# A selective scan whose chunk groups, prefetch distance and state copies are rearranged

## The chip, the core and the metric

The kernel runs on one core of a Trainium2 chip. The metric is the device time of one execution in microseconds (us), lower is better. The median of three runs of the kernel before is 34833.05 us (34830.49 to 34833.85). Four engines compute: TensorE (PE in the profile, its weight loads PEld), VectorE (DVE), ScalarE (ACT) and GpSimd (POOL). SyncE (SP) issues the DMA transfers. Each engine runs its own list of instructions strictly in order; between engines, an instruction waits on semaphores until what it needs is done.

## The reference

Two layers work on an image batch of 8 x 56 x 56 x 192 in float32. The first (a gated Toeplitz convolution) is not touched. The second is a vision state-space block: a projection to 384 channels, a 3x3 depthwise convolution, and then a selective scan along eight directions over the 3136 pixels, with N = 16 states per channel:

```python
dA = jnp.exp(dl[..., None] * A)
h = dA * h + (dl * ul)[..., None] * bl[:, :, None, :]
y = jnp.einsum('bkdn,bkn->bkd', h, cl)
```

Here `dl` is delta (a softplus of a projection of the pixel), `ul` the pixel, `bl` and `cl` the projected B and C, k the direction. Afterwards the eight directions are added, normalised, gated with silu and projected. The scan is the bulk of the work: 8 images x 8 directions x 3136 steps x 384 channels x 16 states.

## The kernel before

**Units.** For each image the scan stage cuts a direction into 50 chunks of 63 pixels and the 384 channels into three blocks of 128. One chunk of one channel block is a *unit*: 8 x 150 = 1200 units per image, 9600 in all. Units of the three channel blocks are dealt out in turn (block d lags d chunks behind), so the unit before in the same chain, whose last state is needed, is three units back.

**What one unit costs each engine.** PE makes delta*u*B for all states as a product of the turned delta*u with a diagonal image of B (`products`, L723, into one of three PSUM buffers `bx`). ACT makes exp(delta*A) ahead of time (`exps`, L702, 16 instructions per *block*, one for each state, over all the block's chunks at once, into one of four buffers `da`), and copies the chain's last state into the first column of `bx` (`before`, L734, the "state copy"). DVE runs the recurrence (`scan`, L738). POOL multiplies by C (`times_c`, L749, into `hc`). PE adds the 16 states by transposing them onto one another (`sums`, L835, eight instructions per unit, into `yps`); every fourth unit ACT copies `yps` out (L869, tile `yt`, the "output copy"), and SP stores it.

**Groups and blocks.** The chunks of a direction form groups of 8, and a last group of 2 (50 = 6 x 8 + 2). A group's front work is shared: load (`load`), projection on PE and ACT (`project`, `projected`), delta (`steps`, `stepped`, one `softplus` on ACT, L591, which brings another activation table in and the exponential's back, L702 ACT_TABLE_LOAD), and per pair of chunks delta*u on POOL (`product`, L614), its transpose (`turn` on PE, `turned` on ACT: tile `dut`), a copy with halves exchanged (`swapped`: `dus`), the diagonal of B back from DRAM (`diagonal_in`: `bd`) and C broadcast to all partitions (`broadcast`: `cbt`). The 2-chunk group has special functions (`all_steps`, `all_stepped`). A block is the four (in the last group two) chunks of one channel block that share 16 exponentials.

**The order is written out by hand.** A loop runs over steps t, one unit each; at step t the lists of all engines get, in this order: products of unit t+2; the store of earlier outputs; state copies of units t to t+2, as far as not done; sums of unit t-4; the output copy where t is a multiple of 4; planned ACT work; exponentials; the scan of unit t; planned PE work; times C of unit t-1; planned POOL and SP work; more exponentials; at last planned "late" work (the softplus). `plan` sets the steps of the front work relative to the group's first unit f. Exponentials are dealt out by a budget: each step adds 2.4 to `credit` (a debt stays, a surplus lapses), an exponential costs 0.4, a state copy 0.2, an output copy 0.35, planned ACT work 0.5, a softplus 3.0. While credit is left, exponentials are issued as far as their `da` buffer is free by the order of units (`may_exp`). Without regard to credit, all that remain of a block are issued at the step before its first unit (`must_exp`):

```python
            def may_exp(t):
                if not exps:
                    return False
                P = exps[0][0]
                return P.i < 4 or t > blocks[P.i - 4].end

            def must_exp(t):
                return bool(exps) and t >= exps[0][0].first - 1
```

## Time and profile before

| | us |
|---|---|
| median of three runs | 34833.05 |
| profiled execution | 34832.71 |
| its span | 34830.9 |
| PE busy | 30277.1 (87%) |
| DVE busy | 23676.0 (68%) |
| ACT busy | 22543.9 (65%) |
| POOL busy | 22154.0 (64%) |

The span divides into a first layer (up to about 3650 us) and eight rounds, one per image, of a scan stage and a shorter stage around it. In the trace the scans of the third image run from 11519 to 14950 us, 3431 us for 1200 units; the eight images are alike. PE's busy time counts pipelined matrix products by modelled ends, so its 87% says less than it seems to. The page's line of granted clocks (PEclk) is the share of full speed at which TensorE was allowed to run; in this kernel it moves between half and full in stretches of some microseconds.

### The profile page before, as it was taken

The numbers are of one execution on the slowest core, as the hardware profiler recorded it, in microseconds if no ns is written. First come the engines' busy times: TensorE is split into PE (matmuls) and PEld (weight loads), VectorE is DVE, ScalarE is ACT, GpSimd is POOL, SyncE is SP. The second block draws the span as 40 slices with busy tenths as digits, with TensorE's granted clock in tenths as the row PEclk, the third lists the DMA queues.
The fourth block names the chain that finished last, engine by engine and source line by source line (L and its number), as shares of the span: only waits on it lengthen the run. The fifth ranks groups of instructions, "written<-read, shape, count | busy, mean of one in ns | idle before, by whom it ended". The sixth has DMA issues, their size and how long they took to land. (4 is left out here: it accounts for less than half of the span.)

```text
span 34830.9 us, 473357 instructions
## 1 busy us (share of the span) xinstructions
PE 30277.1 (87%) x156976; PEld 16476.7 (47%) x156976; DVE 23676.0 (68%) x13460; ACT 22543.9 (65%) x58955; POOL 22154.0 (64%) x11592
## 2 busy tenths in 40 slices
PE   8999888888888888888888888888888888888888
PEld 5555444444444444444444444444444444444444
DVE  3443577747776677747776677747776677747776
ACT  2332577737775677737775577747775577737775
POOL 0000687838875588738885588838885588837885
PEclk9999999989999899989999899989999899989999
DMA  3222444444444444444444444444444444444445
GB/s 76 58 65 54 115 126 129 127 129 127 127 129 135 121 127 127 128 129 127 127 127 137 122 127 126 129 129 127 127 126 136 122 128 127 127 129 128 127 127 145
DMA packets 5635667, 4228.55 MB, mean 121 GB/s; under 512 B 3712080, under 2 KB 5007888, under 8 KB 5625680
## 3 DMA queue, kind: packets, MB, share of 16 engines
q1 hardware_dynamic: 5600080, 4191.04, 45.6%
q8 instruction: 1262, 20.68, 0.2%
q10 hardware_dynamic: 33152, 7.23, 0.2%
q14 instruction: 1173, 9.61, 0.1%
HBM read 3389.38 MB, written 507.38 MB: 112 GB/s over the span
## 5 line engine op out<-in xcount | busy, mean ns | idle before, releaser
L738 DVE TENSOR_TENSOR_SCAN h<-da,bx 128x1024 f32<-128x1024 f32 x9600 | 21246.8, 2270 | 6552.5 <-ACT bx L734 4705.1
L749 POOL TENSOR_TENSOR hc<-h,cbt 128x1008 f32<-128x1008 f32 x9600 | 20512.7, 2169 | 4271.5 <-DVE h L738 3956.8
L702 ACT ACTIVATE da<-delta,A_logs 128x252 f32<-128x252 f32 (+1 forms) x39936 | 16435.2, 489 | 5.6
L723 PE MATMUL bx<-bd,dus 63*128 63x504 f32 x19200 | 11288.7, 670 | 2682.7 <-DVE h L738 2679.7
L835 PEld LDWEIGHTS yps<-ident,hc 128*126 128x126 f32 x76800 | 8599.6, 145 | 7854.7 <-issue 4818.3
L723 PE MATMUL bx<-bd,dut 63*128 63x504 f32 x19200 | 11296.7, 670 | 81.6 <-DVE h L738 66.7
L835 PE MATMUL yps<-ident,hc 128*126 128x128 f32 x76800 | 10942.6, 288 | 266.2 <-ACT yt L869 235.7
L723 PEld LDWEIGHTS bx<-bd,dus 63*128 63x128 f32 x19200 | 2995.8, 195 | 4689.6 <-DVE h L738 3606.0
L734 ACT COPY bx<-h 128x16 f32<-128x16 f32 x9408 | 1695.0, 181 | 4555.2 <-PE bx L723 3257.6
L723 PEld LDWEIGHTS bx<-bd,dut 63*128 63x128 f32 x19200 | 2995.9, 195 | 1271.5 <-issue 920.5
L614 POOL TENSOR_TENSOR du<-delta,xs 128x378 f32<-128x378 f32 x1600 | 1587.1, 992 | 1550.1 <-ACT bx L734 1377.5
L425 POOL MEMSET xp<- 128x58 f32 x12 | 1.3, 188 | 3409.8 <-DMA bd<-none 3409.7
L869 ACT COPY yt<-yps 126x256 f32<-126x256 f32 x2400 | 891.0, 371 | 1917.0 <-PE yps L835 1794.0
L989 POOL COPY xo<-xp 128x672 f32<-128x672 f32 x98 | 70.5, 749 | 2849.7 <-ACT xp L972 2849.7
L547 PE MATMUL px<-xs,xpw 128*64 128x504 f32 (+1 forms) x2688 | 1367.9, 593 | 195.2 <-DMA xs<-xo 195.2
L578 PE MATMUL pd<-pxs,dtw 13*128 13x504 f32 x2304 | 1294.4, 641 | 17.8 <-ACT delta L587 10.7
L623 PE MATMUL pt<-ident,du 128*128 128x128 f32 x4800 | 816.5, 279 | 411.1 <-POOL du L614 405.5
L965 PE MATMUL pc<-xp,dg 128*128 128x448 f32 x2646 | 1019.6, 538 | 0.0
L972 ACT ACTIVATE xp<-pc,conv_b 128x448 f32<-128x448 f32 x147 | 93.5, 636 | 1345.8 <-PE pc L965 1345.6
L1109 DVE SCALAR_TENSOR_TENSOR y<-xc,dsum,ysum 128x224 f32<-128x224 f32 x336 | 125.4, 443 | 1128.6 <-PE ysum L1090 1128.6
L623 PEld LDWEIGHTS pt<-ident,du 128*128 128x128 f32 x4800 | 559.5, 142 | 529.0 <-POOL du L614 517.2
L631 ACT COPY dut<-pt 128x384 f32<-128x384 f32 x1600 | 766.2, 479 | 25.3 <-PE pt L623 24.9
(137 smaller groups left out, 16295.3 us busy)
## 6 DMA issues: line engine op xcount, KB each, us to landing
cbt<-cd SPq DMA_DIRECT2D x1600, 1008.0 KB
bd<-bd SPq DMA_DIRECT2D x3200, 256.0 KB
dus<-dut SPq DMA_DIRECT2D x3200, 96.0 KB
yk<-yt SPq DMA_DIRECT2D x3584, 84.0 KB
yt<-yt SPq DMA_DIRECT2D x9408, 31.5 KB
xs<-xo SPq DMA_DIRECT2D x384, 756.0 KB
xo<-xo SPq DMA_DIRECT2D x168, 672.0 KB
bd<-pxs SPq DMA_DIRECT2D x3200, 3.9 KB
```

The source lines that it names most:

```text
L547: nc.tensor.matmul(self.px[:, : self.n], weights[self.k][0][:, d], self.xs[:, d], start=(d == 0), stop=(d == NB - 1),)
L578: nc.tensor.matmul(self.pd[:, : self.n], weights[self.k][1][:, d * 128 : (d + 1) * 128], self.pxs[0 : R + 1], start=True, stop=True,)
L614: nc.gpsimd.tensor_mul(self.du[:, :, :, :W], self.delta[:, :, part].rearrange("p d (c t) -> p d c t", t=W), xs[:, :, part].rearrange("p d ...
L623: nc.tensor.transpose(self.pt[:, d * 128 : (d + 1) * 128], self.du[:, d].rearrange("p c t -> p (c t)"), ident,)
L702: yield nc.scalar.activation(da[:, : self.nc, n, 1:], src.rearrange("p (c t) -> p c t", t=W), AF.Exp, scale=an[:, G.k, self.d, n : n + 1],)
L723: nc.tensor.matmul(self.bx[:, r, :, 1:], G.dut[p][q ^ r][rows, self.d * 128 : (self.d + 1) * 128], G.bd[p][rows, q, :, :W], start=True, st ...
L734: nc.scalar.copy(self.bx.rearrange("p r n t -> p (r n) t")[:, :, 0], src)
L738: nc.vector.tensor_tensor_scan(self.h.rearrange("p n t -> p (n t)"), das[self.P.i % 4][:, self.slot].rearrange("p n t -> p (n t)"), self.b ...
L749: nc.gpsimd.tensor_tensor(hc, self.h[:, :, 1:], self.G.cb[self.c // 2][:, :, q * W : (q + 1) * W], ALU.mult)
L835: nc.tensor.matmul(yps[:, t // 4 % 2, t // 2 % 2], lhsT=hcs[t // 2][:, n].rearrange("p c t -> p (c t)"), rhs=ident, start=(n == 0), stop=( ...
L869: nc.scalar.copy(y, yps[:, s // 4 % 2])
L965: nc.tensor.matmul(pc, dg[:, d, j, :], xp[:, d, t * RT + dy : t * RT + dy + RT, dx : dx + HW], start=(j == 0), stop=(j == 8),)
```

## The change

- The groups become 8, 6, 8, 6, 8, 6, 8 chunks (SIZES) instead of six of 8 and one of 2; a block is half a group, four or three chunks. The special functions of the 2-chunk group go. The exponentials of a direction become 42 blocks of 16 instead of 39, in all 43,008 instructions instead of 39,936, over 252 or 189 elements a partition instead of 252 or 126.
- delta*u, its transpose, exchanged copy and diagonals are planned three steps earlier (s = f - 11 + 6p instead of f - 8 + 6p); the pool `blk` that holds them gets four buffers instead of three. The exchanged copy is issued one step after the diagonals instead of before them. The softplus is at f - 14 instead of f - 10; the projection at f - 27 instead of f - 24 (f - 30 for the 2-chunk group).
- The state copy is issued one unit ahead instead of two: at step t for units t and t+1, after the sums, and after up to two exponentials that are issued whatever the credit. Ahead of a softplus, the copies of the next two units are issued.

```diff
-NG = -(-NC // GC)
+SIZES = (8, 6, 8, 6, 8, 6, 8)
-            blk = st.enter_context(tc.tile_pool(name="blk", bufs=3))
+            blk = st.enter_context(tc.tile_pool(name="blk", bufs=4))
...
                 def softplus(self):
-                    v = self.delta.rearrange("p d l -> p (d l)")
-                    nc.scalar.activation(v, v, AF.Softplus)
+                    nc.scalar.activation(self.delta, self.delta, AF.Softplus)
...
                 def plan(self, at):
                     f = self.first
-                    if self.last:
-                        x = f - 30
-                        at("PE", f - 24, self.all_steps)
-                        at("late", f - 23, self.all_stepped)
-                    else:
-                        x = f - 24
-                        for d, s in enumerate((f - 18, f - 16, f - 12)):
-                            at("PE", s, self.steps, d)
-                            at("ACT", s + 1, self.stepped, d)
-                        at("late", f - 10, self.softplus)
-                    at("SP", x - 12, self.load)
+                    x = f - 27
+                    at("SP", f - 35, self.load)
...
-                    at("SP", x + 3, self.to_dram)
+                    at("SP", x + 4, self.to_dram)
+                    for d, s in enumerate((f - 21, f - 19, f - 15)):
+                        at("PE", s, self.steps, d)
+                        at("ACT", s + 1, self.stepped, d)
+                    at("late", f - 14, self.softplus)
                     for p in range(self.npr):
-                        at("SP", x + 3 + p, self.diagonal_out, p)
-                        s = f - 8 + 6 * p
+                        at("SP", x + 4 + p, self.diagonal_out, p)
+                        s = f - 11 + 6 * p
                         at("POOL", s - 1, self.product, p)
                         at("PE", s, self.turn, p)
                         at("ACT", s + 1, self.turned, p)
-                        at("SP", s + 1, self.swapped, p)
                         at("SP", s + 1, self.diagonal_in, p)
+                        at("SP", s + 2, self.swapped, p)
...
                 def __init__(self, G, s, d):
-                    self.nc = min(SC, G.nch - s * SC)
+                    self.nc = G.sc
...
+            def befores(t, n):
+                nonlocal credit
+                for U in units[max(t, 0) : max(t + n, 0)]:
+                    if not U.ready and (U.prev is None or U.prev.h is not None):
+                        U.before(U.prev)
+                        credit -= 0.2
+
...
-                for i in range(t, t + 3):
-                    U = unit(i)
-                    if U is not None and not U.ready and (U.prev is None or U.prev.h is not None):
-                        U.before(U.prev)
-                        credit -= 0.2
                 s = t - 4
                 if unit(s) is not None:
                     if s % 2 == 0:
...
                         sums(s - 1, 1)
                         hcs.pop(s // 2)
+                for i in range(2):
+                    if may_exp(t):
+                        one_exp()
+                befores(t, 2)
...
                 while credit > 0.2 and may_exp(t):
                     one_exp()
+                if ("late", t) in plan:
+                    befores(t + 1, 2)
                 credit -= 3.0 * do("late", t)
```

## The prediction

> **What bounds the kernel now.** I read the costliest groups first, then busy time by windows inside one scan stage, then the timeline at its worst and at a quiet place.

> ```profile
> L738 DVE TENSOR_TENSOR_SCAN h<-da,bx 128x1024 f32<-128x1024 f32 x9600 | 21246.8, 2270 | 6552.5 <-ACT bx L734 4705.1
> L734 ACT COPY bx<-h 128x16 f32<-128x16 f32 x9408 | 1695.0, 181 | 4555.2 <-PE bx L723 3257.6
> L869 ACT COPY yt<-yps 126x256 f32<-126x256 f32 x2400 | 891.0, 371 | 1917.0 <-PE yps L835 1794.0
> ```

> DVE's scan is the spine of a stage; of its 6552 us of idle time 4705 end with ScalarE's state copy, so the copy arrives late.

> ```profile
> 11948.00:12062.00 114.00, 83.64 (x374) 43.29 (x373) 64.51 (x30) 65.10 (x178) 69.45 (x36) 0.84 0.34 94
> 12130.00:12376.00 246.00, 238.97 (x1306) 127.89 (x1306) 222.39 (x101) 214.09 (x579) 226.21 (x117) 1.00 0.56 149
> ```

> Columns: PE, PEld, DVE, ACT, POOL busy (count), granted clock, DMA share, GB/s. Around a change of direction 30 scans take 114 us (3.8 us a unit, clock 0.84); in the middle 101 take 246 us (2.44, clock 1.00) with PE busy 97%. A direction takes 3431/8 = 428.9 us; at 2.44 throughout it would be 366. So 63 us per direction, 4.0 ms in 64, are lost around the 2-chunk group. There the timeline reads:

> ```profile
> 11982.66 0.19 ACT L734 COPY bx<-h 128x16 f32<-128x16 f32 x1 [2.06 <-PE bx L723]
> 11982.79 0.57 ACT L587 COPY delta<-pd 128x504 f32<-128x504 f32 x1
> 11983.26 5.64 ACT L702 ACTIVATE da<-delta,A_logs 128x252 f32<-128x252 f32 x14
> 11988.81 0.17 ACT L734 COPY bx<-h 128x16 f32<-128x16 f32 x1
> 11988.99 8.82 DVE L738 TENSOR_TENSOR_SCAN h<-da,bx 128x1024 f32<-128x1024 f32 x4 [7.77 <-ACT bx L734]
> 11991.33 1.20 PE L723 MATMUL bx<-bd,dus 63*128 63x504 f32 x1 [4.58 <-DVE h L738]
> 11993.31 1.97 PE L835 MATMUL yps<-ident,hc 128*126 128x128 f32 x8
> 11996.44 1.10 PE L835 MATMUL yps<-ident,hc 128*126 128x128 f32 x8
> ```

> Fourteen exponentials that were overdue go out in one run (5.64 us; (5.64 - 0.50)/13 = 0.395 us each), DVE waits 7.77 us, PE in turn 4.58 us, and then works at half speed (sums 1.97 instead of 1.10 us). So the disease is a *run of exponentials ahead of a scan*; the idle PE and its lower clock make it worse. Last, the quiet stretch:

> ```profile
> 4521.20 1.09 PE L835 MATMUL yps<-ident,hc 128*126 128x128 f32 x8
> 4522.33 0.37 ACT L869 COPY yt<-yps 126x256 f32<-126x256 f32 x1 [0.82 <-PE yps L835]
> 4511.48 1.28 ACT L591 ACT_TABLE_LOAD   x1
> 4512.77 1.46 ACT L591 ACTIVATE delta<-delta 128x1512 f32<-128x1512 f32 x1
> 4514.41 15.54 DVE L738 TENSOR_TENSOR_SCAN h<-da,bx 128x1024 f32<-128x1024 f32 x7 [1.95 <-ACT bx L734]
> ```

> The output copy starts 0.04 us after the sums *of its own step* end (4521.20 + 1.09), although they write the other half of `yps`: it stands behind them. A softplus costs DVE 1.95 us.

> **The change, part by part.** Times below are per direction unless said otherwise; E is the end of a scan.

> *Front work three steps earlier, four buffers, order of its DMAs.* Nothing is added: 25 pairs a direction as before, two transfers each for diagonals and exchanged copy. They have little to give: idle time on all engines that a diagonals' transfer ended around `bx` is 64 us in the whole run. On SP the diagonals pass the exchanged copy, which stands one step longer; both have seven steps (over 15 us) before use. On POOL delta*u goes two steps behind the softplus instead of one, so its 2.8 to 3.9 us wait there goes; POOL's demand (2.14 + 0.99/6 = 2.30 us a unit) is under PE's. I take 0, bounds -1 us a direction (64/64) to +1 (one late transfer, 0.56 us issue).

> *Exponentials.* 252 elements cost 0.395; 126 elements 0.295 (five in 1.57); so 189 about 0.345 (estimate between the rows). 384 x 0.395 + 288 x 0.345 = 251 us against 576 x 0.395 + 48 x 0.295 = 242: 9 us more ACT work, beside a PE that needs 2.07 + 0.31 = 2.38 us a unit (products 1.05, sums 1.02; projections, delta and transposes 7.4 us in 24 units). Cost 0 as work. Their *place* is what counts.

> *The budget.* In 18 units of a 6-group: 96 exponentials x 0.4 + 18 x 0.2 + 4.5 x 0.35 + 7 x 0.5 + 3 = 50.1 against 18 x 2.4 = 43.2. An 8-group: 52.3 against 57.6. A pair loses 1.6, and a debt stays. So the budget never allows anything; all that runs ahead is the forced two a step, and the rest falls due at once. The program of the changed kernel shows this all the way (copies C with unit number, then what ACT does up to the next; S softplus, Y output copy):

> ```
> C192 dut 2exp | C193 Y 8exp 2exp | C194 delta 2exp | C195 2exp | C196 delta 2exp | C197 Y 8exp 2exp
> C200 delta | C201 S 2exp Y 8exp 2exp | C202 2exp ...   (8-group)
> C218 delta | C219 S 4exp | C220 2exp | C221 Y 8exp 2exp | C222 dut 14exp 2exp   (6-group)
> ```

> Runs of six and more stood before about nine times a direction; now each of 42 blocks begins with 8 or 14 overdue ones (10 or fewer behind a softplus). For half of the 8-groups (the alignment shifts by two with each 6-group) they stand behind the output copy.

> *State copy one unit ahead.* Before, a run of exponentials stood behind the copy of unit t+2, which waits for the scan t-1; now behind that of t+1, which waits for t-2. So a run has one scan more of cover, 2.2 us. That is all that the move gives; with 42 runs a direction instead of nine it is used up, and behind an output copy, which waits for products of t+2 as before, it does not exist.

> *Eight behind the output copy* (unit t+1, step t). From E(t-1): 0.1 to PE, product 1.05, sums 1.09, 0.04, copy 0.27 to the next instruction, eight exponentials 3.27, 0.09 to the scan: 5.9. Then the scans t+1 to t+3, 2.26 + 2 x 2.2 = 6.7 (2.2: eleven scans in 24.30 us), until the next such E: 12.6 us per four units, where 2.44 gives 9.8.

> *Eight without it.* The copy, one ahead, waits for E of three units back: 0.1 + 1.16 + 0.13 + 3.27 + 0.09 = 4.75, then two scans 4.5: 9.2; PE's 9.5 is longer. With the projections' steps in a row, 10.0.

> *Softplus in an 8-group.* Two copies stand ahead of it now, the second waits for its products and holds the softplus behind it by 1.4; and the next scan needs it *and* ten exponentials: 1.4 + 4.0 (two loads and the softplus) + 3.95 + 0.3 = 9.6, then 4.5: 14.1 per four units.

> *6-group.* Softplus, 30 exponentials x 0.345 and small copies fall in one chain of five units: 1.4 + 4.1 + 10.3 + 0.9 = 16.7 against 11.0. A second chain: 1.4 + 2.8 + 0.8 + 0.4 + 5.5 + 0.2 = 11.1 against 6.6. 18 x 2.2 + 5.7 + 4.5 = 49.8, with output copies 50.5.

> *Half clock.* Without it: 2 x (5 x 12.6 + 14.1) + 2 x (5 x 9.5 + 14.1) + 3 x 50.5 = 428.9, by chance what a direction takes now. But PE idles: after the product and sums of t+1 up to 3.9 us behind the output copy, 5 us at a softplus, 3.9 and 4.5 in a 6-group; before, 4.58 was enough. Its price from the run of 14: 0.1 + 1.16 + 0.13 + 0.47 + 5.6 + 0.1 = 7.6 after the E at 11979.0 (four scans from 11972.40 on, of which the third ended there) would be 11986.6; the scan came 2.4 later. Bounds 0 and 2.4 for each; I take 1.2 per output-copy four (work of PE next to it often fills the gap), 1.5 per softplus, 2 per chain of a 6-group: 2 x (5 x 13.8 + 15.6) + 2 x (5 x 10 + 15.6) + 3 x 54.5 = 464. That is +35 us, x 64 = 2240 us on the profiled 34832.7 (the median is 0.3 more): **37,070 us**.

> [...]

> **Rivals.**
> - *No throttling* (clock 1.00 as in the middle): 428.9 a direction, about 34,830. For it: waits at PE of 1 to 2 us in the middle left the clock at 1.00. Against it: 4.58. With errors of +-9 us a direction, 34,250 to 35,400.
> - *Faster: the output copy does not hold the eight.* If it found its sums long done, eight would cost 10.0 everywhere: 464 - 2 x 19 = 426; without the clock's loss then (-25) 401, so 33,050. It decides from 2.8 us less per such four. Against it: 1794 of the copy's 1917 us idle end with the sums.
> - *Faster: the middle's pace everywhere*, 366 + 3 a direction: 31,000. Speaks for it that the 2-chunk group is gone; against it the runs of eight and fourteen.
> - *Worse throttling*: every event pays 2.4, output-copy groups at 15 per four units: 490, so 38,750.

> **How the numbers follow.** Main case 0.70 (35,400 to 38,600); no throttling 0.11 (faster 0.04, same 0.02, slower 0.05); output copy free 0.08; middle's pace 0.04; worse throttling 0.07. Faster by over 0.2% (about what a measurement of this kernel can tell from no change) 0.16, same 0.02, slower 0.82. The range 34,600 to 38,600 leaves out the two faster cases and most of the worst.

> **What would show it.** Right: DVE's idle time spread over whole stages instead of around direction changes; most of it ended by exponentials (`da`) rather than by the state copy; runs of eight at once after an output copy; PEclk below 9 tenths throughout; four units at 12.5 to 15 us in every second 8-group. Wrong: clock 1.00 and 2.4 us a unit in 8-groups; or the output copy starting right after its state copy.

## The result, and the profile after

The changed kernel takes 39,644.4 us (median of four runs, 39,637.2 to 39,664.8) against 34,832.3 for the kernel before (34,830.5 to 34,833.9). The ratio is 1.138, with a 95% interval of 1.136 to 1.140. Slower was predicted (chance 0.82), but the size was not: 37,070 us was forecast and the range ended at 38,600. A scan stage of one image takes 4030 us instead of 3430, or 504 us a direction instead of 429; the prediction had 464.

The page of the kernel after, its costliest groups (busy time and mean ns of one, then the idle time of the engine just before them and what ended most of it), with the line of granted clocks:

```profile
span 39636.9 us, 475157 instructions
PE 32472.0 (82%) x156976; PEld 17579.7 (44%) x156976; DVE 23680.0 (60%) x13460; ACT 22984.7 (58%) x62219; POOL 22269.5 (56%) x11592
PEclk9998888888888888888888888888888888888888
...
L714 DVE TENSOR_TENSOR_SCAN h<-da,bx 128x1024 f32<-128x1024 f32 x9600 | 21257.8, 2269 | 11361.9 <-ACT da L678 9433.6
L853 ACT COPY yt<-yps 126x256 f32<-126x256 f32 x2400 | 888.2, 370 | 6335.9 <-PE yps L813 6329.9
L710 ACT COPY bx<-h 128x16 f32<-128x16 f32 x9408 | 1653.7, 176 | 2550.0 <-PE bx L699 2376.6
```

The busy time of DVE is what it was (23,680 us); ACT has 441 us more work. What grew is DVE's idle time ahead of the scans: 11,362 us instead of 6552, 4810 more, which is the whole difference of the two times. Before, most of it ended with the state copy; now 9434 of it ends with an exponential (`da`). The output copy, which sits on ACT ahead of such exponentials, waited 1794 us for its sums before; now it waits 6330.

Two groups of 8 chunks of the third image by windows (PE, PEld, DVE, ACT, POOL busy with counts, granted clock, DMA share, GB/s), the first with its blocks' starts behind output copies, the second without, and then the whole scan stage:

```profile
13334.00:13431.00 97.00, 77.22 (x315) 40.27 (x316) 52.92 (x24) 51.16 (x140) 54.86 (x28) 0.76 0.34 80
13493.00:13563.00 70.00, 60.97 (x300) 32.31 (x301) 52.85 (x24) 49.24 (x137) 52.31 (x28) 0.90 0.49 119
12718.00:16750.00 4032.00, 3284.33 (x15614) 1737.25 (x15615) 2657.49 (x1202) 2666.26 (x7440) 2755.41 (x1405) 0.87 0.41 107
```

Twenty-four scans take 97 us in the one group and 70 in the other. In the first the clock is at 0.76. Over the run (from the start of the scan three units ahead of a group to the same place of the next group, means):

| us per group | predicted, full clock | predicted in all | measured |
|---|---|---|---|
| 8 chunks, output copy ahead of the block starts | 77.1 | 84.6 | 93.7 |
| 8 chunks, without | 61.6 | 65.6 | 70.4 |
| 6 chunks | 50.5 | 54.5 | 59.0 |

A direction has two, two and three of them. (In the prediction's sum without the half clock four units of the second kind stand at 9.5 us, in its whole sum at 10.0; it gave the 0.5 to the projections' steps, so 2.5 of the 4.0 us between 61.6 and 65.6 are no clock.) The shortfall of 41 us is 2 x 9.1 + 2 x 4.8 + 3 x 4.5: it lies in all three kinds, and most in the first. The timeline shows the kind that lost most: four units, from one output copy to the next (called a *four* below), of the first group (start, duration, engine, in brackets the idle time before it and what ended it):

```profile
13345.09 0.37 ACT L853 COPY yt<-yps 126x256 f32<-126x256 f32 x1 [2.78 <-PE yps L813]
13345.36 4.06 ACT L678 ACTIVATE da<-delta,A_logs 128x252 f32<-128x252 f32 x10
13348.72 8.82 DVE L714 TENSOR_TENSOR_SCAN h<-da,bx 128x1024 f32<-128x1024 f32 x4 [5.49 <-ACT da L678]
13351.06 1.21 PE L699 MATMUL bx<-bd,dus 63*128 63x504 f32 x1 [3.11 <-DVE h L714]
...
13353.05 1.97 PE L813 MATMUL yps<-ident,hc 128*126 128x128 f32 x8
13354.94 1.62 PE L577 MATMUL pd<-pxs,dtw 13*128 13x378 f32 x2
13356.50 1.21 PE L699 MATMUL bx<-bd,dut 63*128 63x504 f32 x1
...
13358.48 1.97 PE L813 MATMUL yps<-ident,hc 128*126 128x128 f32 x8
...
13361.62 1.10 PE L813 MATMUL yps<-ident,hc 128*126 128x128 f32 x8
...
13362.76 0.37 ACT L853 COPY yt<-yps 126x256 f32<-126x256 f32 x1 [3.97 <-PE yps L813]
13363.02 4.06 ACT L678 ACTIVATE da<-delta,A_logs 128x252 f32<-128x252 f32 x10
```

The output copy, ten exponentials of which the scan needs the first eight, the scan 3.63 us after the copy: that is the predicted chain. PE restarts after 3.1 us of idleness and 2.34 us after the scan's start. Its three products, three sums and a delta projection then stand between it and the next output copy, all up to the last product and sums at half speed (sums 1.97 instead of 1.09). That copy comes 11.70 us after the restart, and the next such scan (13366.38) 17.66 us after the first, where the prediction had 13.8.

### The profile page after: what moved, and what is told of

It is laid out like the page before. It is cut to its first block, busy times and chain, and to the rows that moved or that the text cites. A ratio compares the mean times of both kernels' runs of the same rounds, so it can differ in the third digit from the quotient of the medians.

```text
span 39636.9 us, 475157 instructions
## 1 busy us (share of the span) xinstructions
PE 32472.0 (82%) x156976; PEld 17579.7 (44%) x156976; DVE 23680.0 (60%) x13460; ACT 22984.7 (58%) x62219; POOL 22269.5 (56%) x11592
## 5 line engine op out<-in xcount | busy, mean ns | idle before, releaser
L678 ACT ACTIVATE da<-delta,A_logs 128x252 f32<-128x252 f32 x43008 | 17071.6, 474 | 5.4
L699 PE MATMUL bx<-bd,dus 63*128 63x504 f32 x19200 | 12353.3, 728 | 4953.1 <-DVE h L714 4945.7
L813 PEld LDWEIGHTS yps<-ident,hc 128*126 128x126 f32 x76800 | 9318.2, 153 | 8623.7 <-issue 6599.5
L699 PE MATMUL bx<-bd,dut 63*128 63x504 f32 x19200 | 12361.1, 728 | 859.9 <-DVE h L714 845.5
L813 PE MATMUL yps<-ident,hc 128*126 128x128 f32 x76800 | 11784.0, 302 | 176.5 <-ACT yt L853 163.1
L699 PEld LDWEIGHTS bx<-bd,dus 63*128 63x128 f32 x19200 | 3210.9, 209 | 6203.1 <-DVE h L714 5560.1
L699 PEld LDWEIGHTS bx<-bd,dut 63*128 63x128 f32 x19200 | 3211.2, 209 | 3077.5 <-issue 1769.7
L577 PE MATMUL pd<-pxs,dtw 13*128 13x504 f32 (+1 forms) x2688 | 1597.9, 678 | 36.0 <-ACT dut L612 18.2
L586 ACT COPY delta<-pd 128x504 f32<-128x504 f32 (+1 forms) x1344 | 713.4, 531 | 1116.9 <-PE pd L577 1116.8
```

The lines of the kernel that those rows point to most:

```text
L577: nc.tensor.matmul(self.pd[:, : self.n], weights[self.k][1][:, d * 128 : (d + 1) * 128], self.pxs[0 : R + 1], start=True, stop=True,)
L678: yield nc.scalar.activation(da[:, : self.nc, n, 1:], src.rearrange("p (c t) -> p c t", t=W), AF.Exp, scale=an[:, G.k, self.d, n : n + 1],)
L699: nc.tensor.matmul(self.bx[:, r, :, 1:], G.dut[p][q ^ r][rows, self.d * 128 : (self.d + 1) * 128], G.bd[p][rows, q, :, :W], start=True, st ...
L813: nc.tensor.matmul(yps[:, t // 4 % 2, t // 2 % 2], lhsT=hcs[t // 2][:, n].rearrange("p c t -> p (c t)"), rhs=ident, start=(n == 0), stop=( ...
```

## The experiments

The prediction's own theory (the letter A in the quoted expectations, each of which says what it stands for) is: a budget that stays in debt lets exponentials fall due eight and fourteen at a time, these runs hold the scan up, most of all behind an output copy, and TensorE, idle meanwhile (3.1 us in the four above), loses half its clock (0.50 granted for 10.24 us there, 0.76 in the mean of the group). Its rivals are the parts of the change themselves (earlier front work, new place of the state copy, size of groups). Times of 34,814 to 34,881 us were measured for the kernel before beside these runs; each ratio is to those.

### The budget's debt taken away

An exponential is charged by its size (0.3 for three chunks, 0.4 for four), so that an 18-unit group sums to 50.1 - 96 x 0.1 = 40.5 against its 43.2, and the debt of the run-in (the steps ahead of the first unit) is dropped. The two edits were not timed apart, but the program's own loop tells how many of an image's 5376 exponentials fall due without credit: 2938 in the changed kernel, 2875 with the debt dropped alone (it comes back), 322 with the charge by size alone, 301 with both. So nearly all of it is the charge.

```diff
-                credit -= 0.4
+                credit -= 0.1 * exps[0][0].nc
...
-                credit = min(credit, 0.0) + 2.4
+                credit = min(credit, 0.0) * (t > 0) + 2.4
```

> The changed kernel, with one thing else: an exponential instruction is charged by its size (0.4 for four chunks, 0.3 for three) and the debt is cleared at step 0, so that the budget holds and exponentials are issued ahead (4 to 7 a step) instead of falling due eight and fourteen at a time. Theory A (overdue runs of exponentials, sharpened by PE's lower clock): the stalls of 3.5 to 9.5 us before block starts vanish, the clock is back near 1.00 in the stage, a direction takes 366 to 390 us instead of 504: 30,800 to 32,300 us. Rival B (the grouping itself, or the front work three steps earlier, costs the time through more blocks, 3072 more exponentials and crowded PE steps): it stays over 37,000. Rival C (the state copy issued late is the cost, since it leaves one scan of cover): over 36,000.

Measured: 32,218.8 us, 0.925 of before (0.924 to 0.926), clock 0.965 over the run. With all the rest of the change in place, two numbers in the budget are worth 7426 us. The groups take 61.3, 60.3 and 47.5 us. The line of its scan, from its page:

```profile
L714 DVE TENSOR_TENSOR_SCAN h<-da,bx 128x1024 f32<-128x1024 f32 x9600 | 21278.6, 2270 | 3913.1 <-ACT bx L710 1445.9
```

Of the 11,362 us of DVE's idle time 3913 are left, and exponentials no longer end most of it. The budget is the cause of the loss, not the new groups as such.

### The parts of the change alone

The front work three steps earlier, with four buffers and the new order of its DMAs, on the kernel before; the 2-chunk group's projection moves with it.

```diff
-            blk = st.enter_context(tc.tile_pool(name="blk", bufs=3))
+            blk = st.enter_context(tc.tile_pool(name="blk", bufs=4))
...
-                        x = f - 24
-                        for d, s in enumerate((f - 18, f - 16, f - 12)):
+                        x = f - 27
+                        for d, s in enumerate((f - 21, f - 19, f - 15)):
...
-                        at("late", f - 10, self.softplus)
+                        at("late", f - 14, self.softplus)
...
-                        s = f - 8 + 6 * p
+                        s = f - 11 + 6 * p
...
-                        at("SP", s + 1, self.swapped, p)
                         at("SP", s + 1, self.diagonal_in, p)
+                        at("SP", s + 2, self.swapped, p)
```

> The kernel before with the front work alone moved: delta*u, transpose, exchanged copy and diagonals three steps earlier in four buffers, exchanged copy behind the diagonals, projection and delta three and softplus four steps earlier (the 2-chunk group's projection and delta three earlier too); groups, state copies and budget as before. Theory A: the waits lie with runs of exponentials, which stay; 34,830 within 300 us. Rival B (the crowded or shifted front work costs, or its earlier transfers gain): more than 500 us off.

Measured: 34,920.9 us, 1.0023 (1.0013 to 1.0033). That is 1.2 us a direction (0.7 to 1.8 by the interval), about the bound of 1 that the prediction gave, and nothing beside the 75 in question.

The new place of the state copy alone, on the kernel before:

```diff
-                for i in range(t, t + 3):
-                    U = unit(i)
-                    if U is not None and not U.ready and (U.prev is None or U.prev.h is not None):
-                        U.before(U.prev)
-                        credit -= 0.2
...
+                for i in range(2):
+                    if may_exp(t):
+                        one_exp()
+                befores(t, 2)
...
+                if ("late", t) in plan:
+                    befores(t + 1, 2)
```

> The kernel before with the new order of state copies alone (one unit ahead, behind the sums and two forced exponentials, two copies ahead of a softplus); groups of 8 and 2 and front work as before. Theory A: the nine long runs of a direction remain but have one scan more of cover (2.2 us each and part of the clock's loss), the softplus stall of 2 us goes: 25 to 45 us a direction less, 32,000 to 33,300 us. Rival C (the later copy costs): slower than 34,830.

Measured: 33,612.6 us, 0.9649 (0.9633 to 0.9665). The gain is 19 us a direction. The prediction said one scan of cover, 2.2 us, for each long run of exponentials, of which the kernel before has about nine: 20 us. The range on record had been set deeper, and the time missed it by 300 us. That 19 and 20 agree does not show the price per run, since the edit also brings the two forced exponentials and the copies ahead of a softplus, and the trace has fewer long runs: 464 of six and more instead of 544.

The opposite: the changed kernel with the old order of copies, with neither the forced exponentials ahead of the copies nor the early copies at a softplus.

```diff
+                befores(t, 3)
                 s = t - 4
...
-                for i in range(2):
-                    if may_exp(t):
-                        one_exp()
-                befores(t, 2)
...
-                if ("late", t) in plan:
-                    befores(t + 1, 2)
```

> The changed kernel with the state copies issued as before (units t to t+2 ahead of the sums, no two forced exponentials, no copies ahead of the softplus); groups, front work and buffers as changed. The program then issues nearly all blocks as runs of sixteen. Theory A: a run of sixteen costs 1.4 + 6.3 + 0.2 - 2.2 = 5.7 us and 2.5 for the clock, 42 times a direction: 330 + 42 x 8.2 = 675 us, so 50,000 us (45,000 to 54,000). Rival C (the later state copy is what costs): at or under 39,640, towards 35,000.

Measured: 50,393.1 us, 1.447 (1.444 to 1.450). Without the two forced ones a step, all sixteen exponentials of a block fall due at once, 2328 times, behind a copy that waits for a scan. From its page:

```profile
PEclk9997777877777777877778777777778777787777
...
L714 DVE TENSOR_TENSOR_SCAN h<-da,bx 128x1024 f32<-128x1024 f32 x9600 | 21201.3, 2268 | 22172.6 <-ACT bx L710 21999.2
```

DVE waits longer than it works. So the new order of copies with its two forced exponentials, which the prediction credited with 2.2 us a run, is worth 10,700 us in the changed kernel; the harm comes from what stands beside it. How much of that is the copies' place and how much the forced exponentials was not tried, nor were the new groups without the earlier front work.

Then the budget without the new groups: on the kernel before, and on the kernel with the new copies. The diff is that of the first experiment.

> The kernel before with nothing but the charge by size (0.4 for four chunks, 0.2 for two) and the debt cleared at step 0. The program still has some ten runs of more than five exponentials a direction, as the kernel before, since around the 2-chunk group 96 exponentials must pass in six units. Theory A (the number of runs sets the time): 34,830 within 500. Rival G (the wrong charge alone is what costs, before too): under 33,500.

Measured: 34,042.7 us, 0.977 (0.975 to 0.979). The expected "no change" missed by 290 us. The trace has no fewer runs of six and more (640, before 544), but only 8 of fourteen and more instead of 128. So the kernel before had some debt of its own; that it came from the 2-chunk groups is likely and not shown.

> The kernel before with the new order of state copies and with exponentials charged by size (0.4 for four chunks, 0.2 for two) and the debt cleared at step 0; groups of 8 and 2 as before. The program still has about eight runs of seven and more in a direction, around the 2-chunk group, where 96 exponentials must pass in six units; the run with the copies alone had nine to ten and took 33,613. Theory A: the count of runs sets the time: 33,000 (32,400 to 33,600), over the 32,219 of the kernel with even groups and the same charge. Rival E (the grouping in 8 and 6 gives nothing once the budget holds): 32,220 or less.

Measured: 33,412.2 us, 0.959 (0.957 to 0.961), as expected. Beside the 32,218.8 of the first experiment this prices the new groups with a budget that closes: they *save* 1193 us, the earlier front work included. Measured singly, the parts are thus worth about +79 us (front work, on the kernel before), -1220 (copies, on the kernel before) and, with the budget mended, -1190 (groups with the front work). In the changed kernel the budget as it was costs 7426.

### The output copy

In the changed kernel the exponentials due, and the planned ACT work ahead of them, are issued ahead of the output copy:

```diff
+                credit -= 0.5 * do("ACT", t)
+                while must_exp(t):
+                    one_exp()
                 s = t - 8
...
-                credit -= 0.5 * do("ACT", t)
-                while must_exp(t):
-                    one_exp()
```

> The changed kernel with the output copy issued behind the overdue exponentials of its step instead of ahead of them; the runs of eight stay. Theory A: where the output copy stood ahead of a run (every second 8-group, 93.7 us now, and its neighbour of six, 60.7), the groups become like the others (70.4 and 57.2): 64 x (2 x 23.3 + 1.5 x 3.5) = 3300 us less, about 36,300 (35,700 to 37,200). Rival D (the output copy only happens to stand there; the clock and the run length make the difference): within 500 us of 39,640.

Measured: 35,579.1 us, 1.0215 (1.0195 to 1.0236), 121 us below the range expected. The groups take 66.6 us (those that had taken 93.7), 70.2 and about 55.5; the clock is 0.93. From its page:

```profile
L714 DVE TENSOR_TENSOR_SCAN h<-da,bx 128x1024 f32<-128x1024 f32 x9600 | 21248.7, 2269 | 7318.9 <-ACT da L678 4521.5
L856 ACT COPY yt<-yps 126x256 f32<-126x256 f32 x2400 | 872.8, 364 | 3727.8 <-PE yps L813 3717.6
```

The 27 us per group are the price of standing behind the output copy, what it does to the clock included; the groups without one stay where they were. All of it is still slower than before: the runs of due exponentials cost time behind a state copy too.

### What half the clock costs

Idle transposes (into a quarter of `yps` that the next sums overwrite; nothing reads them) fill PE's gaps. First 16 of them in each fourth unit, everywhere:

```diff
+            def filler(t):
+                for n in range(N):
+                    nc.tensor.matmul(
+                        yps[:, t // 4 % 2, 1],
+                        lhsT=hcs[t // 2][:, n].rearrange("p c t -> p (c t)"),
+                        rhs=ident,
+                        start=(n == 0),
+                        stop=(n == N - 1),
+                        is_transpose=True,
+                        skip_group_check=True,
+                    )
...
                         sums(s - 1, 1)
+                        if s % 4 == 1:
+                            filler(s - 1)
```

> The changed kernel with more work: behind the sums of every fourth unit PE does sixteen transposes (2.05 us) into a quarter of yps that nothing needs and the next sums overwrite; they fall where PE waits up to 3.9 us for a scan behind a run of eight. Nothing else is changed. Theory A1 (PE's idle gaps of over 3 us halve its clock, and the slow products and sums behind them make the output copy and so the next run late): the clock rises from 0.877 of the run, 8-groups with the output copy ahead of the run fall from 93.7 to about 80 us, the others rise by up to 4: about 38,000 us (37,200 to 39,000) in spite of the added work. Rival D1 (the clock shown is a mere symptom, the time is all in waits): 4.1 us of added work per eight units behind a PE that is late anyway, 40,000 to 41,500.

Measured: 39,589.9 us, 1.136 (1.135 to 1.138). This lies between the ranges of both sides and settles nothing: the clock rose from 0.877 to 0.933, the groups of the first kind fell from 93.7 to 85.8 us, but those without an output copy rose from 70.4 to 73.2 and those of 6 from 59.0 to 61.7. Fillers that stand where PE isn't idle cost what others win.

So, 20 of them only where a run of more than five stands behind an output copy, 1016 times:

```diff
+                        if hot:
+                            filler(s - 1)
...
+                    due += 1
+                hot = due > 5 and t % 4 == 0
```

> The changed kernel with twenty idle transposes (2.6 us of added PE work) only where a run of more than five exponentials has just been issued behind an output copy: 1016 times, in the gap of 3.1 to 3.9 us in which PE there waits for a scan. The filler at every fourth unit raised the clock of these 8-groups from 0.787 to 0.904 and took them from 93.7 to 85.8 us, and cost the other groups as much. Theory A2 (the clock's price at a run behind the output copy is 3 to 5 us, not the 1.2 of the prediction): clock over 0.95 there, 8-groups with the output copy 76 to 82 us (about 13 us per four units), the others unchanged: 37,400 us (36,900 to 38,300). Rival D1 (the clock has no part in it): 39,400 or more, since PE only gets more work.

Measured: 37,983.8 us, 1.090 (1.089 to 1.092). Work that computes nothing makes the changed kernel 4.2% faster. Its timeline over the same four units (copied here to the restart and the next output copy):

```profile
12913.43 2.35 PE L827 MATMUL yps<-ident,hc 128*126 128x128 f32 x20
12914.36 8.82 DVE L714 TENSOR_TENSOR_SCAN h<-da,bx 128x1024 f32<-128x1024 f32 x4 [5.42 <-ACT da L678]
...
12916.70 0.69 PE L699 MATMUL bx<-bd,dus 63*128 63x504 f32 x1 [0.93 <-DVE h L714]
...
12917.75 1.09 PE L813 MATMUL yps<-ident,hc 128*126 128x128 f32 x8
...
12923.85 0.37 ACT L869 COPY yt<-yps 126x256 f32<-126x256 f32 x1 [2.79 <-PE yps L813]
...
12927.48 4.46 DVE L714 TENSOR_TENSOR_SCAN h<-da,bx 128x1024 f32<-128x1024 f32 x2 [4.30 <-issue]
```

The restart comes 2.34 us after the scan and the scan 3.63 us after the output copy, as in the kernel after. Between them lie 7.15 us instead of 11.70. The filler ends before the restart (12913.43 + 2.35), so it is not on the path. Half the clock cost this four 4.55 us: it takes 13.12 instead of 17.66, and the same products, sums and projection lie in both. The whole group takes 81.0 instead of 93.7; the others stay within a microsecond (70.1 and 58.5).

Last, fillers also behind a softplus's step and after runs of more than eleven, 1432 in all:

```diff
+                    if hot:
+                        filler(s - s % 2)
...
+                    due += 1
+                hot = due > 5 and (t % 4 == 0 or soft or due > 11)
+                soft = ("late", t) in plan
```

> The kernel after with 20 idle transposes (2.6 us at full clock in the run with such a filler behind the output copy) after every run of more than five exponentials that stands behind an output copy, after every softplus's step and after every run of more than eleven: some 1,430 fillers instead of 1,016. Theory A3 (the rest of the shortfall, in the eights without an output copy and in the groups of six, is the half clock too): the clock over 0.96, eights without a copy 70 to about 66 us, sixes 57 to 60 to about 54, the time about 36,700 us (36,100 to 37,500), under the 37,984 of the run with the filler behind the output copy alone. Rival R3 (only the fours behind an output copy paid for the clock; the rest is the sizes of the waits themselves): 37,800 us or more, since the added transposes are TensorE work of 416 x 2.6 = 1,080 us that then stands partly on the path.

Measured: 37,389.9 us, 1.072 (1.071 to 1.074), clock 0.959. The time is inside A3's range, at its upper end, and the clock just under it. The groups are not where A3 had them: 81.4, 68.5 and 56.3 us, with about 66 and about 54 expected of the latter two. The clock's records say why. In the kernel after, the half clock holds for 40.2, 12.0 and 9.0 us of a group; with these fillers for 5.6, 5.6 and 0.3. In the groups of 6 hardly any is left, and they still take 56.3 us: what remains there is the size of the waits at full clock, as the rival had it. Both theories hold a part.

### A better kernel

With the budget mended, the output copy was moved to either end of its step. At the end of the step, ahead of the softplus:

```diff
-                s = t - 8
-                if unit(s) is not None and s % 4 == 0:
-                    y = pre.tile([2 * W, 2, 128], F32, name="yt")
-                    nc.scalar.copy(y, yps[:, s // 4 % 2])
...
                 while credit > 0.2 and may_exp(t):
                     one_exp()
+                s = t - 8
+                if unit(s) is not None and s % 4 == 0:
+                    y = pre.tile([2 * W, 2, 128], F32, name="yt")
+                    nc.scalar.copy(y, yps[:, s // 4 % 2])
```

> The changed kernel with exponentials charged by size and, besides, the output copy issued at the end of its step behind all of the step's exponentials. With the charge alone ACT idles 3016 us ahead of output copies. Theory A: that wait is covered by exponentials, 300 to 1000 us less than 32,219: 31,200 to 31,900. Rival F (PE's own work of 2.38 us a unit, 357 us of the 388 a direction takes, leaves no more): within 150 us of 32,219; or PE now waits for the output copy before its next sums and it is slower.

Measured: 31,157.3 us, 0.8941 (0.8928 to 0.8954), the fastest of all and slightly better than expected. Ahead of the sums of its step, where its own sums are long done:

```diff
                 stores = []
+                s = t - 8
+                if unit(s) is not None and s % 4 == 0:
+                    y = pre.tile([2 * W, 2, 128], F32, name="yt")
+                    nc.scalar.copy(y, yps[:, s // 4 % 2])
...
                 s = t - 4
```

> The changed kernel with exponentials charged by size, and the output copy issued ahead of the sums of its step, so that it waits for the sums of the step before only; those of its own step then wait for the copy. Theory A (what matters is that the copy doesn't hold up ACT): between 31,000 and 32,000, near the 31,157 of the copy at the end of the step. Rival H (PE, now held by ACT before its sums, loses more than ACT gains): over 32,219.

Measured: 31,226.0 us, 0.8965 (0.8947 to 0.8983). The two are alike: what matters is that the copy no longer stands between the sums of its step and the exponentials. The page of the faster one, and a group of 8 of it by windows:

```profile
PE 29162.1 (94%) x156976; PEld 15964.2 (51%) x156976; DVE 23707.1 (76%) x13460; ACT 22834.4 (73%) x62219; POOL 22183.2 (71%) x11592
PEclk9999999999999999999999999989999999989999
...
L714 DVE TENSOR_TENSOR_SCAN h<-da,bx 128x1024 f32<-128x1024 f32 x9600 | 21285.3, 2270 | 2826.2 <-ACT bx L710 1735.7
```

```profile
11082.00:11141.00 59.00, 57.76 (x316) 30.91 (x316) 53.08 (x25) 52.81 (x146) 55.06 (x29) 1.00 0.59 145
```

PE is busy 57.8 of 59 us at a clock of 1.00, the bound that the quiet stretch of the kernel before had shown; a scan stage takes 2966 us, 371 a direction. The half clock is granted eight times in its scan stages, 1277 times in those of the kernel after.

## Why the prediction was wrong

**The direction and the mechanism** held, each part with a run. The debt: mending the budget takes 7426 us away. Runs of eight and fourteen at the start of every block, where long runs had stood about nine times a direction: DVE's idle time ends with exponentials in 9434 of 11,362 us. The chain behind the output copy: 3.63 us from copy to scan in the trace, as the sum of 0.27 + 3.27 + 0.09 had it; taken out from under the copy, the group falls from 93.7 to 66.6. The front work: 1.2 us a direction for a predicted 0 +-1. The state copy: 19 us a direction for nine runs at 2.2, which may be chance, as said above. Four of the five signs that the prediction named as right are in the profile after; the fifth is exceeded, since the fours of every second 8-group take 14.5 to 18.2 us, not 12.5 to 15. The rival cases (no throttling; output copy free; the middle's pace) are out. The case called worse throttling, 38,750 us, came nearest and was still 900 us short.

One sum behind the debt was wrong without harm. "A pair loses 1.6, and a debt stays" counts as many groups of 6 as of 8, but a direction has four of 8 and three of 6: 4 x 52.3 + 3 x 50.1 = 359.5 against a credit of 360. The debt does not grow; it is never worked off. In the program's loop it stands at 5.4 after the first direction and at 4.1 after the seventh.

**The size** failed in two steps, worth 41 us a direction together. To part them I use the last run with fillers. There the fillers removed 34.6, 6.4 and 8.8 us of half clock per group and gave 12.3, 1.9 and 2.7 us of time, about 0.3 us for each. Scaled to what half clock was left, the groups would take some 79.4, 66.9 and 56.2 us at full clock. This is an estimate; where fillers were themselves on the path it puts too much on the waits and too little on the clock.

| us per group | waits: predicted, estimated | half clock: predicted, estimated |
|---|---|---|
| 8 chunks behind output copies | 77.1, 79.4 | 7.5, 14.3 |
| 8 chunks without | 64.1, 66.9 | 1.5, 3.5 |
| 6 chunks | 50.5, 56.2 | 4.0, 2.8 |
| sum of a direction | 434, 461 | 30, 44 |

The fours without an output copy stand here at the 10.0 us of the prediction's whole sum. By that its "without it" would be 434 instead of 428.9.

*First step that failed: "Eight without it" and "6-group", some 23 us of the 41* (2 x 2.8 + 3 x 5.7). For the eights without an output copy the prediction began the chain at the state copy, "4.75, then two scans 4.5: 9.2; PE's 9.5 is longer". In the trace of the kernel after, a four of that kind at full clock reads:

```profile
13507.13 0.69 PE L699 MATMUL bx<-bd,dus 63*128 63x504 f32 x1
...
13508.18 1.09 PE L813 MATMUL yps<-ident,hc 128*126 128x128 f32 x8
...
13509.31 0.37 ACT L853 COPY yt<-yps 126x256 f32<-126x256 f32 x1 [2.49 <-PE yps L813]
13509.57 0.90 ACT L678 ACTIVATE da<-delta,A_logs 128x252 f32<-128x252 f32 x2
...
13510.38 0.18 ACT L710 COPY bx<-h 128x16 f32<-128x16 f32 x1
13510.49 0.47 ACT L586 COPY delta<-pd 128x378 f32<-128x378 f32 x1
13510.85 0.90 ACT L678 ACTIVATE da<-delta,A_logs 128x252 f32<-128x252 f32 x2
...
13511.66 0.18 ACT L710 COPY bx<-h 128x16 f32<-128x16 f32 x1
13511.76 4.07 ACT L678 ACTIVATE da<-delta,A_logs 128x252 f32<-128x252 f32 x10
...
13515.13 8.82 DVE L714 TENSOR_TENSOR_SCAN h<-da,bx 128x1024 f32<-128x1024 f32 x4 [1.55 <-POOL xs L538]
```

An output copy, here that of two steps before, still starts the chain. Behind it ACT goes without a pause through two forced exponentials, a state copy, the delta copy, two more forced ones, the next state copy and the eight: 5.82 us from the output copy to the scan. (The bracket names a POOL instruction on `xs`, but the eighth exponential ends where the scan starts: 13511.76 + 7 x 0.40 + 0.50 = 13515.06.) With 2.26 us of the scan ahead of it and 2.29 from that scan's end to the output copy the four takes 10.37. So the forced exponentials, which the prediction counted as work beside PE, lay on the path: four of them, 1.6 us, with 0.4 of the delta copy. Over the run the fours of such a group take 11.9, 10.5, 14.7 (softplus), 12.3, 11.3 and 9.9 us, where 10 and 15.6 were forecast. In the 6-groups the prediction priced two chains and 0.7 us for all output copies. The timeline of the last run with fillers, at full clock, shows two eights behind output copies inside one such group, and a run of sixteen after the second; of its first fourteen the scan at 12867.53 needs the last:

```profile
12846.25 0.37 ACT L870 COPY yt<-yps 126x256 f32<-126x256 f32 x1 [2.89 <-PE yps L813]
12846.52 3.54 ACT L678 ACTIVATE da<-delta,A_logs 128x189 f32<-128x189 f32 x10
...
12849.46 6.64 DVE L714 TENSOR_TENSOR_SCAN h<-da,bx 128x1024 f32<-128x1024 f32 x3 [3.38 <-issue]
...
12858.34 0.37 ACT L870 COPY yt<-yps 126x256 f32<-126x256 f32 x1 [1.16 <-PE yps L813]
12858.61 3.54 ACT L678 ACTIVATE da<-delta,A_logs 128x189 f32<-128x189 f32 x10
...
12861.55 2.29 DVE L714 TENSOR_TENSOR_SCAN h<-da,bx 128x1024 f32<-128x1024 f32 x1 [2.79 <-ACT da L678]
...
12862.53 5.61 ACT L678 ACTIVATE da<-delta,A_logs 128x189 f32<-128x189 f32 x16
12867.53 2.29 DVE L714 TENSOR_TENSOR_SCAN h<-da,bx 128x1024 f32<-128x1024 f32 x1 [3.70 <-ACT da L678]
```

Over that run, in half of these groups six of the 18 scans start 2.1 to 4.3 us late; in the other half, whose alignment is shifted by two, three start about 1.3 late and two 3.8 and 7.4. The block starts hold DVE one by one, not in two chains. A smaller part, 2 x 2.3 us, is the four behind the output copy, 13.1 at full clock for "12.6": a delta projection (0.83 us from its start to the next product) lies in the PE chain that the prediction built of products and sums alone.

*Second step that failed: "Half clock ... Bounds 0 and 2.4 for each; I take 1.2 per output-copy four", some 14 us of the 41* (2 x 6.8 + 2 x 2.0 - 3 x 1.2). The single four measured 4.55, outside the bounds. It is a bad one: over the run a group of that kind has 40.2 us of half clock, 6.7 a four, and pays at least 12.7 us (93.7 to 81.0), by the estimate above 14.3, or 2.4 a four. That is the upper bound, twice what was taken. The bound itself was read off badly. It came from a scan of the kernel before that was 2.4 us later than the prediction's chain, and here is what PE did ahead of it:

```profile
11974.74 0.85 PE L723 MATMUL bx<-bd,dus 63*128 63x504 f32 x1 [4.67 <-DVE h L738]
...
11976.38 1.97 PE L835 MATMUL yps<-ident,hc 128*126 128x128 f32 x8
...
11980.46 1.11 PE L578 MATMUL pd<-pxs,dtw 13*128 13x504 f32 x2
```

A delta projection stands in that chain too (1.04 us to the next product, at 11981.50) and was left out of the sum. The clock was at half for 3.41 us alone, which can explain at most half of that, 1.7. In the four of the kernel after it was at half for 10.24 us, and PE's whole way from the restart to the start of the last product ahead of the output copy lies in that stretch. By windows (columns as above), first the stretch of the kernel before, then that of the kernel after:

```profile
11975.14:11978.55 3.41, 3.41 (x14) 1.84 (x12) 3.41 (x2) 0.36 (x2) 3.30 (x2) 0.50 0.00 0
13350.58:13360.82 10.24, 9.76 (x28) 5.08 (x30) 6.96 (x4) 2.68 (x9) 7.65 (x5) 0.50 0.41 124
```

So the price was taken at a short stretch, with a projection in it that it did not name; the stretches of the kernel after last 6.5 us in the mean (8243 us in 1277). What makes a stretch long is not shown. Waits of PE inside it are seldom the reason: in 1211 of the 1277 stretches of the kernel after PE made no pause of over 0.3 us between the end of the gap and the end of the stretch.

What remains open: how the 27 us of waits divide among the other fours, what the fillers cost where they are not clear of the path, and what sets the length of a stretch at half clock.

**Gaps and the clock.** For the length of a gap the prediction had two readings: 4.58 us of idleness had been enough for a drop, and waits of 1 to 2 us in the middle had left the clock at 1.00. The kernel after shows what lies between, and that gaps under 2 us were not safe in it either. In its scan stages a new drop of the clock (begun in the gap or within 1.5 us behind it) followed 1016 of 1035 gaps of 3 us and more, and also 260 of 511 gaps of 1.5 to 3 us, 67 of these among the 230 under 2.

## What to carry to other kernels

Where a hand-made budget deals out work, check that it leaves something over in each kind of period: one that only just balances never works off a debt, and the debt turns "as early as possible" into "all at once, when due". Two small edits of a budget were worth 7426 of 39,644 us here. Price an in-order engine's chain from the last thing it had to wait for, with everything queued between (the small copies and "free" early work too; 5.82 us from output copy to scan in the four at full clock above), not from the instruction that looks nearest. When another engine idles meanwhile, ask how much of *its* chain then runs at half clock before the loop comes round again: here a gap of 3.11 us was followed by 10.24 us at half clock, which cost 4.55.
